# Turning the row maxima of both query halves with one product, and moving that product inside a layer-2 slot

## The chip, the core and the metric

One core of one Trainium2 chip runs the whole program. The metric is device time in microseconds (us); the median of the timed runs is compared. The engines named below are PE (TensorE, with its weight loads shown as PEld), DVE (VectorE), ACT (ScalarE), POOL (GpSimd) and SP (SyncE, which issues most DMAs).

## The reference

Two cross-attention layers, one after the other, on x of shape (16, 256, 320) with a context of shape (16, 256, 512). Each layer has 20 heads of 16 channels. The last 4 context tokens are image tokens, the first ones text. Layer 1 treats 77 tokens as text and all the others as image tokens; layer 2 treats 252 as text and 4 as image.

```python
# layer 1, cut
q = x @ Wq;  k_text = text @ Wk;  v_text = text @ Wv          # text = context[:, :77]
probs = softmax(q_h @ k_h^T * scale);  text_out = probs @ v_h
scores = q_h @ ip_k_h^T * scale                                # ip = context[:, 77:]
text_probs = softmax(q @ k_text^T * scale)                     # over all heads at once
sem = (text_probs @ text) @ ip^T * scale
ip_probs = softmax(scores + 0.5 * sem) * spatial_mask
out = (text_out + ip_probs @ ip_v_h) @ Wout + bout + x
# layer 2, cut (text = context[:, :252], ip = context[:, 252:])
probs_t = softmax(q @ k_t^T * scale);  text_out = probs_t @ v_t
qsem = l2norm(probs_t @ text);  sem = qsem @ l2norm(ip)^T
probs_ip = softmax(q @ k_ip^T * scale + 0.5 * sem) * spatial_mask
out = (text_out + probs_ip @ v_ip) @ W_out + b_out + x
```

Every softmax over tokens needs the row maximum of its scores per query and head; that is what this change is about.

## The kernel before

The work is cut into groups of 4 heads of one batch: 16 batches x 5 groups = 80 groups per layer (NS = 80), and one group is handled in one *slot*. Slots 0 to 79 are layer 1 (`slot0`), 80 to 159 layer 2 (`slot1`). The 256 queries of a batch are worked in two halves of 128 (t = 0, 1).

For a group the kernel computes the scores twice. The first time queries lie on the partitions (`score0`, L772; in layer 2 the second loop of `both1`, L922), only to get the row maxima with DVE (L773 and L774 for the text and image part in layer 1, L923 in layer 2). The second time tokens lie on the partitions (`turned0`, L795; in layer 2 the first loop of `both1`, L917), and there the maxima enter as extra rows of the stacked operand Q, so that ACT's exponential (L798, L929) can read the scores out of PSUM with the maximum already subtracted. To become rows of Q, the maxima have to be turned: a product with the identity puts them on a few partitions (`maxima0`, L780; `maxima1`, L955), ACT copies that to the tile mt (L782, L957), and a small DMA issued by ACT writes mt into Q (L783, L959). The tile mn with the maxima has one part per query half, and each half has a product of its own.

A layer-1 slot k runs, in PE's order: `maxima0` for group k+1, the scores of group k+2 for half 0, `turned0` of group k for half 0, fill, `attend0` of group k-1 (L833, the weighted values), the scores of group k+2 for half 1, `turned0` for half 1, fill. A layer-2 slot k runs: `both1` half 0 (L917 for group k, L922 for group k+2), `attend1` of group k-2 (L988 and L990, into the values' bank pv of tag P), `both1` half 1, then the norm products of group k-1 (`norm1`, L975, in four portions with fill between them), and at its end `maxima1` for group k+2. POOL multiplies and subtracts on the probabilities (L801, L966).

*Fill* is everything that is not per group: projections of queries, keys and values (L260, L632), the semantic scores of layer 1 (L690 to L719), closing a batch (`close0`, `close1`), loading and splitting weights (weights1 to weights8). These are generators, and the table `STEPS` says for each of their steps at which time (counted in slots, relative to the batch or to the start of layer 2) it is run; `fill` runs the steps that are due. PE's order is always the written one. In layer 1 a scheduler orders ACT, DVE, POOL and SP; in layer 2 only SP's queue.

PSUM has 8 banks: 2 of tag T (turned scores), 1 of tag P (the values' bank), 3 of tag X (all else, taken in a ring by `bank()`), and S (2 banks, one tile) for the scores. `late` keeps back an instruction until `settled` or `release`, `hold` begins such a stretch.

Of the kernel before, what the change touches and what calls it, by code (L numbers as in the profile page):

```python
# [9 lines left out]
FR = mybir.dt.float32r  # L10
# [6 lines left out]
B = 16  # L17
# [22 lines left out]
LEAD = 4  # L40

# [8 lines left out]
def xattn2(  # L50
# [714 lines left out]
    def score0(k, t):  # L765
        Q, K = QK[k]
        if t == 0:
            maxes[k] = buf("mn", [128, 2, 2, 4], FR, bufs=2)
        mn = maxes[k]
        sp = scores()  # L770
        for h in range(4):
            mm(sp[:, h], Q[: XROW + T0, h, t * 128 : (t + 1) * 128], K[: XROW + T0, h], start=True, stop=True)  # L772
        nc.vector.tensor_reduce(mn[:, t, 0], sp[:, :, :T0], axis=AX.X, op=ALU.max)  # L773
        anchor(nc.vector.tensor_reduce(mn[:, t, 1], sp[:, :, T0:], axis=AX.X, op=ALU.max))  # L774

    def maxima0(k, queue=nc.scalar):
        Q, mn = QK[k][0], maxes[k]
        mp = bank()
        for t in range(2):
            mm(mp[:8, t * 128 : (t + 1) * 128], mn[:, t].rearrange("p a h -> p (a h)"), ident_r, start=True, stop=True)  # L780
        mt = buf("mt", [8, S], FR)
        casts.append(nc.scalar.copy(mt, mp[:8, :S]))  # L782
# [120 lines left out]
    def both1(k, t):  # L903
# [3 lines left out]
        if a:  # L907
            if t == 0:
                maxes[k + 2] = buf("mn", [128, 4, 4], FR, bufs=2)[:, :2]
# [8 lines left out]
        if a:  # L918
# [4 lines left out]
            anchor(nc.vector.tensor_reduce(maxes[k + 2][:, t], sp[:, :, :T1], axis=AX.X, op=ALU.max))  # L923
# [27 lines left out]
    def maxima1(k):  # L951
        mn = maxes[k]
        mp = bank()
        for t in range(2):
            mm(mp[:4, t * 128 : (t + 1) * 128], mn[:, t], ident_r, start=True, stop=True)  # L955
        mt = buf("mt", [8, S], FR)[:4]
        nc.scalar.copy(mt, mp[:4, :S])  # L957
# [35 lines left out]
    def slot1(k):  # L993
        last = k - 1 if NS < k <= 2 * NS else None
        mine = k < 2 * NS
        if k == NS:
# [4 lines left out]
        summed = []  # L1001
# [3 lines left out]
        yield lambda: both1(k, 1)  # L1005
        if last:
# [19 lines left out]
        yield lambda: maxima(k + 2)  # L1026
# [153 lines left out]
    def first_keys():  # L1180
# [5 lines left out]
    STEPS = {  # L1186
        "k1": (-7, -6.2, -6.2, -5, -4.2, -3.4,),
        "t1": (-3.2, -2.2, -2.2, -1.4, -0.2,),
        "o1": (-7, -6.8, -6, -5.8, -4, -3.4,),
        "i1": (6.8, 7.6, 7.6, 8.8, 9.4, 9.6, 10.6, 10.8, 10.8, 12.2,),  # L1190
        "c1": (12.8, 12.8, 13.4, 14, 14, 15.8,),
        ("i1", B - 2): (6.6, 7, 7.2, 7.2, 7.8, 8, 8.6, 9.2, 9.2, 9.6,),
        ("c1", B - 2): (9.8, 11.8, 11.8, 12.2, 12.4, 12.4,),
        ("i1", B - 1): (6.8, 7.6, 7.8, 10, 10, 10, 11, 11, 11.2, 12,),
        ("c1", B - 1): (12.2, 13, 13, 13.2, 13.4, 16,),
# [16 lines left out]
        ("c0", B - 1): (5.8, 5.8, 6.4, 7, 7.2, 8,),  # L1212
# [257 lines left out]
```

## Time and profile before

| | |
|---|---|
| timed runs | 1476.69 us median, 1475.23 to 1477.35 |
| profiled execution, first to last instruction | 1475.7 us span; its own time is not listed apart from the runs above |
| PE busy | 97% of the span |
| DVE, POOL, ACT busy | 79%, 78%, 65% |
| granted TensorE clock, mean | 0.993 |
| DMA | 211.78 MB, 144 GB/s on average |

The profile is of one execution. Busy times are sums over the span; matmuls overlap with each other, so for PE the time from the start of one instruction to the start of the next says more than the length of one. The "idle before" of a row is time in which the engine waited, with the event that ended it. Shapes like 128*8 128x128 in a matmul's row are the stationary side and the moving side.

### The profile page before, as it was taken

To read this page: it belongs to the slowest core of one execution; us is meant where nothing else is said; L and a number is where in the kernel's file an instruction comes from. 1 tells how busy PE (TensorE), PEld (TensorE's weight loads), DVE (VectorE), ACT (ScalarE), POOL (GpSimd) and SP (SyncE) were. 2 spreads that over 40 slices of the span, in tenths; PEclk is the share of its full clock that TensorE was granted. 3 is DMA by queue.
4 is the path that set the end of the run, shared out by engine and by line. 5 is a ranking of instruction groups with operands and counts; after the bars stand their busy time and mean duration, and the time that the engine had idled before them with its cause. 6 is when DMAs were issued, how large, how long until landed. Compare 5 with 4: busy or idle time off the path is not lost.

```text
span 1475.7 us, 35302 instructions
## 1 busy us (share of the span) xinstructions
PE 1433.6 (97%) x12438; PEld 1186.7 (80%) x12438; DVE 1166.0 (79%) x2569; ACT 956.5 (65%) x2074; POOL 1151.8 (78%) x1173
## 2 busy tenths in 40 slices
PE   6899999999999999799999999999999999999998
PEld 6788888888888878687778887888888888888865
DVE  5487676777677787967888888888888888888897
ACT  5577676767676776756666566656665666566553
POOL 4179797979797877987788877787778877887785
PEclk9999999999999999999999999999999999999999
DMA  6756565656656577565434433543354345433511
GB/s 196 194 160 184 134 184 141 184 143 165 162 154 164 144 195 205 140 184 158 138 102 140 146 119 101 161 146 102 118 161 146 89 131 161 135 101 116 150 32 50
DMA packets 230667, 211.78 MB, mean 144 GB/s; under 512 B 56314, under 2 KB 217116, under 8 KB 230492
## 3 DMA queue, kind: packets, MB, share of 16 engines
q1 hardware_dynamic: 229222, 208.56, 50.3%
q8 instruction: 99, 1.62, 0.5%
q10 hardware_dynamic: 1270, 0.98, 0.2%
q14 instruction: 76, 0.62, 0.1%
HBM read 122.07 MB, written 86.44 MB: 141 GB/s over the span
## 4 chain that ended last, share of the span: by engine, by line
PE 86%; DMA 4%; DVE 3%; POOL 3%; ACT 2%; issue 1%; SPq 0%; ACTq 0%; DVEq 0%; POOLq 0%
PE X L260 22%; PE X L975 18%; PE X L632 11%; PE P L833 7%; PE S L772 5%; PE P L988 5%; PE T L917 5%; PE T L795 4%; PE S L922 3%; PE P L990 2%; DMA kd<-kst 2%; PE X L1108 1%; POOL P L801 1%; PE X L690 1%; POOL wt L966 1%
## 5 line engine op out<-in xcount | busy, mean ns | idle before, releaser
L801 POOL TENSOR_TENSOR P<-P,rs 128x512 f32<-128x512 f32 x320 | 413.6, 1316 | 140.2 <-ACT P L798 140.2
L975 PE MATMUL X<-ctb,gm 128*128 128x512 f32 x1120 | 295.3, 407 | 0.0
L966 POOL TENSOR_TENSOR wt<-P,ctb 128x512 f32<-128x512 f32 x212 | 268.6, 1296 | 0.0
L923 DVE TENSOR_REDUCE mn<-S 128x4 fp32r<-128x1008 f32 x160 | 192.8, 1205 | 81.0 <-PE S L922 79.4
L975 PEld LDWEIGHTS X<-ctb,gm 128*128 128x128 f32 x1120 | 203.6, 190 | 49.4 <-issue 0.4
L798 ACT ACTIVATE P<-T 128x512 f32<-128x512 f32 x320 | 174.7, 593 | 100.5 <-PE T L795 81.0
L978 DVE TENSOR_TENSOR wt<-X,wt 128x512 f32<-128x512 f32 x240 | 159.3, 681 | 4.9 <-PE X L975 4.9
L929 ACT ACTIVATE P<-T 128x512 f32<-128x512 f32 x212 | 115.0, 597 | 54.5 <-PE T L917 41.6
L980 POOL TENSOR_TENSOR wt<-wt 128x512 f32<-128x512 f32 x80 | 103.6, 1295 | 58.3 <-DVE wt L978 58.3
L965 ACT ACTIVATE ctb<-P 128x512 fp32r<-128x512 f32 x212 | 122.5, 625 | 32.7 <-PE X L975 31.1
L774 DVE TENSOR_REDUCE mn<-S 128x4 fp32r<-128x716 f32 x160 | 142.4, 890 | 0.0
L833 PE MATMUL P<-P,vr 128*32 128x256 f32 x1920 | 123.8, 387 | 1.8 <-DVE tmp L850 0.8
L632 PE MATMUL X<-hq,wE 128*128 128x256 f32 x768 | 111.1, 289 | 4.4 <-ACT hq L615 3.9
L260 PE MATMUL X<-cta,wA 128*128 128x252 f32 (+3 forms) x726 | 104.2, 289 | 6.9 <-ACT wA L187 6.8
L632 PE MATMUL X<-ho,wF 128*128 128x256 f32 x768 | 106.6, 284 | 0.9 <-DVE ho L871 0.6
L632 PEld LDWEIGHTS X<-hq,wE 128*128 128x128 f32 x768 | 101.6, 195 | 7.2 <-ACT hq L615 4.4
L260 PEld LDWEIGHTS X<-cta,wA 128*128 128x128 f32 (+1 forms) x726 | 94.4, 191 | 10.7 <-ACT wA L187 7.0
L632 PEld LDWEIGHTS X<-ho,wF 128*128 128x128 f32 x768 | 98.7, 189 | 3.9 <-DVE ho L871 1.0
L844 DVE STREAM_TRANSPOSE nt<-P 128x512 f32<-128x512 f32 x80 | 57.0, 713 | 44.2 <-PE P L833 43.9
L773 DVE TENSOR_REDUCE mn<-S 128x4 fp32r<-128x308 f32 x160 | 74.5, 466 | 21.5 <-PE S L772 21.1
L833 PEld LDWEIGHTS P<-P,vr 128*32 128x32 f32 x1920 | 55.7, 110 | 42.7 <-issue 6.0
L772 PE MATMUL S<-ks,qs 125*128 125x256 f32 x480 | 87.0, 304 | 0.9 <-DVE mn L774 0.8
(223 smaller groups left out, 3279.7 us busy)
## 6 DMA issues: line engine op xcount, KB each, us to landing
qd<-q SPq DMA_DIRECT2D x48, 384.0 KB
kd<-kst SPq DMA_DIRECT2D x66, 256.0 KB
rawc<-in_cT_dram SPq DMA_DIRECT2D x60, 256.0 KB
qs<-qd SPq DMA_DIRECT2D x160, 96.0 KB
ks<-kd SPq DMA_DIRECT2D x160, 96.0 KB
qs<-qd SPq DMA_DIRECT2D x60, 192.0 KB
ks<-kd SPq DMA_DIRECT2D x60, 192.0 KB
qd<-q SPq DMA_DIRECT2D x32, 256.0 KB
```

The source lines that it names most:

```text
L260: last = mm(out, lhs(a, k), rhs(b, k), start=i == 0, stop=i == len(terms) - 1)
L632: mm(pp, w(s, k, slice(m * 128, (m + 1) * 128)), a[:, t], start=i == 0, stop=i == len(terms) - 1)
L772: mm(sp[:, h], Q[: XROW + T0, h, t * 128 : (t + 1) * 128], K[: XROW + T0, h], start=True, stop=True)
L774: anchor(nc.vector.tensor_reduce(mn[:, t, 1], sp[:, :, T0:], axis=AX.X, op=ALU.max))
L798: exp = anchor(nc.scalar.activation(pt, st[p], AF.Exp, scale=SCALE))
L801: anchor(nc.gpsimd.tensor_mul(pt, pt, rs[:, t : t + 1].to_broadcast([128, 2, S])))
L833: mm(pv[32 * s : 32 * s + 32, o : o + S], v[:, vt, h : h + 32], P[k, s // 2][:, t, s % 2], start=vt < 2, stop=vt != 1,)
L923: anchor(nc.vector.tensor_reduce(maxes[k + 2][:, t], sp[:, :, :T1], axis=AX.X, op=ALU.max))
L965: nc.scalar.activation(R[k, u][:, t], P[k, u][:, t], AF.Copy, scale=0.5)
L966: anchor(nc.gpsimd.tensor_sub(W[k, u][:, t], P[k, u][:, t], f(R[k, u][:, t])))
L975: mm(yp, gm[:, gb], R[k, u][:, kt], start=i == 0, stop=i == len(blocks[n]) - 1)
L978: nc.vector.tensor_mul(product, yp, w[:, n])
```

## The change

The maxima of both halves go into one tile mn in which the half is the last, fastest index. One product then turns all of them: its stationary side has 16 columns (8 in layer 2) instead of two products with 8 (4) columns each, its result has 128 columns instead of 256 on twice the partitions, and so have the copy to mt and the source of the DMA. What lands in Q is the same.

In layer 2 the product for group k+1 is now issued in slot k right behind `both1` half 1, where it was issued for group k+2 at the end of slot k. It goes into columns 384 to 511 of the values' bank that `attend1` of the same slot has just filled (columns 0 to 255), and takes no bank of the X ring. Its DMA is no longer kept back.

Besides, the table `STEPS` is moved to the top of the file, and some of its times change.

```diff
     def score0(k, t):
...
-            maxes[k] = buf("mn", [128, 2, 2, 4], FR, bufs=2)
+            maxes[k] = buf("mn", [128, 2, 4, 2], FR, bufs=2)
...
-        nc.vector.tensor_reduce(mn[:, t, 0], sp[:, :, :T0], axis=AX.X, op=ALU.max)
-        anchor(nc.vector.tensor_reduce(mn[:, t, 1], sp[:, :, T0:], axis=AX.X, op=ALU.max))
+        nc.vector.tensor_reduce(mn[:, 0, :, t], sp[:, :, :T0], axis=AX.X, op=ALU.max)
+        anchor(nc.vector.tensor_reduce(mn[:, 1, :, t], sp[:, :, T0:], axis=AX.X, op=ALU.max))
 
     def maxima0(k, queue=nc.scalar):
         Q, mn = QK[k][0], maxes[k]
-        mp = bank()
-        for t in range(2):
-            mm(mp[:8, t * 128 : (t + 1) * 128], mn[:, t].rearrange("p a h -> p (a h)"), ident_r, start=True, stop=True)
-        mt = buf("mt", [8, S], FR)
-        casts.append(nc.scalar.copy(mt, mp[:8, :S]))
+        mp = bank()[:16, :128]
+        mm(mp, mn.rearrange("p a h t -> p (a h t)"), ident_r, start=True, stop=True)
+        mt = buf("mt", [16, 128], FR)
+        casts.append(nc.scalar.copy(mt, mp))
...
-    def maxima1(k):
+    def maxima1(k, into=None):
         mn = maxes[k]
-        mp = bank()
-        for t in range(2):
-            mm(mp[:4, t * 128 : (t + 1) * 128], mn[:, t], ident_r, start=True, stop=True)
-        mt = buf("mt", [8, S], FR)[:4]
-        nc.scalar.copy(mt, mp[:4, :S])
+        mp = bank()[:8, :128] if into is None else into[:8, 384:]
+        mm(mp, mn.rearrange("p c t -> p (c t)"), ident_r, start=True, stop=True)
+        mt = buf("mt", [8, 128], FR)
+        nc.scalar.copy(mt, mp)
...
     def slot1(k):
...
         yield lambda: both1(k, 1)
+        if k > NS:
+            yield lambda: maxima(k + 1, *[x[2] for x in summed])
...
         yield 0.8
-        yield lambda: maxima(k + 2)
         yield lambda: stacks(k + LEAD)
...
-        for b, t, o in (... (d, (-2.4, -1.4, -1, -0.8, -0.4, 0, 1.2), ...)):
+    "s0o": (-2.4, -1.4, -1, -0.8, -0.4, 0.4, 1.6,),
-        "o1": (-7, -6.8, -6, -5.8, -4, -3.4,),
+    "o1": (-7, -6.8, -6, -5.8, -5.4, -3.4,),
```

The other times that change are: the second and third step of the values of even batches (0.2 later); queries 3, values 2, semantic scores 3 and close 0 at the start of layer 1; weights1, weights6, weights3 and weights8 around the end of layer 1; o1 of batch 0; the last batch's c1.

In the rows below, L826, L833, L848, L772, L773 and L686 of the changed file are L772, L780, L795, L718, L719 and L632 of the file before. On PE in layer 1, around the maxima of slot 42, the order before was:

```order
L772 MATMUL S<-ksl,qsl 128x256 x4
L795 MATMUL T<-qs_187,ks_191 128x256 x4
L632 MATMUL X<-hq_293,wE_85 128x256 x8
L780 MATMUL X<-ident_r,mn_556 8x128 x2
L772 MATMUL S<-ks_190,qs_186 128x256 x4
```

and now it is:

```order
L826 MATMUL S<-ksl,qsl 128x256 x4
L848 MATMUL T<-qs_187,ks_191 128x256 x4
L772 MATMUL X<-tph_449,M_333 128x256
L773 MATMUL X<-tph_449,M_333 128x256
L772 MATMUL X<-tph_449,M_333 128x256
L773 MATMUL X<-tph_449,M_333 128x256
L686 MATMUL X<-hq_293,wE_85 128x256 x8
L833 MATMUL X<-ident_r,mn_556 16x128
L826 MATMUL S<-ks_190,qs_186 128x256 x4
```

The four products of the odd batch's last semantic step (tph with M) stood half a slot earlier, ahead of `attend0`; they now stand behind `turned0`, and the pair of turning products has become one.

On PE in layer 2, in slot 114 from `both1` half 1 on, the order before was (ctb and gm are operands of `norm1`, hq and wE of a query projection, cta and wA of a key projection):

```order
L917 MATMUL T<-qs_188,ks_192 128x256 x4
L922 MATMUL S<-ks_190,qs_186 128x256 x4
L975 MATMUL X<-ctb_82,gm 128x512 x4
L632 MATMUL X<-hq_293,wE_85 128x256 x8
L975 MATMUL X<-ctb_82,gm 128x512 x3
L975 MATMUL X<-ctb_83,gm 128x512 x7
L955 MATMUL X<-ident_r,mn_555 4x128 x2
L260 MATMUL X<-cta_80,wA_84 128x252 x6
```

and now it is (L970, L975, L1007, L1027 and L314 of the changed file are L917, L922, L955, L975 and L260 before):

```order
L970 MATMUL T<-qs_188,ks_192 128x256 x4
L975 MATMUL S<-ks_190,qs_186 128x256 x4
L1007 MATMUL P<-ident_r,mn_556 8x128
L1027 MATMUL X<-ctb_82,gm 128x512 x4
L686 MATMUL X<-hq_293,wE_85 128x256 x8
L1027 MATMUL X<-ctb_82,gm 128x512 x3
L1027 MATMUL X<-ctb_83,gm 128x512 x4
L686 MATMUL X<-hq_293,wE_85 128x256 x8
L1027 MATMUL X<-ctb_83,gm 128x512 x3
L314 MATMUL X<-cta_80,wA_84 128x252 x6
```

The turning product has moved from behind the norm products to ahead of them, from a bank of tag X to the values' bank, and one portion of the query projection (step five of o1) has come into this slot from the next.

On ACT in the same slot, from the second half's exponentials on, the order before was:

```order
L929 ACTIVATE P_93<-T 128x512
L929 ACTIVATE P_94<-T 128x512
L640 CAST q_297<-X 128x256
L965 ACTIVATE ctb_82<-P_93 128x512 x2
L965 ACTIVATE ctb_83<-P_94 128x512 x2
L607 ACTIVATE gm<-gm 128x128
L957 CAST mt_196<-X 4x256
L959 DMA qs_186<-mt_196 2x2x256
L562 CAST kst_235<-X 128x252
```

and now it is (L982, L1009, L1011, L694, L1017, L661 and L616 are L929, L957, L959, L640, L965, L607 and L562 before):

```order
L982 ACTIVATE P_93<-T 128x512
L982 ACTIVATE P_94<-T 128x512
L1009 CAST mt_196<-P 8x128
L1011 DMA qs_188<-mt_196 2x4x128
L694 CAST q_297<-X 128x256
L1017 ACTIVATE ctb_82<-P_93 128x512 x2
L694 CAST q_297<-X 128x256
L1017 ACTIVATE ctb_83<-P_94 128x512 x2
L661 ACTIVATE gm<-gm 128x128
L616 CAST kst_235<-X 128x252
```

The copy to mt and its DMA have moved from the slot's end to right behind the exponentials, ahead of the casts to ctb.

More of the change, by code (lines that the diff above doesn't have):

```diff
@@ L908, in both1 @@
             if t == 0:
-                maxes[k + 2] = buf("mn", [128, 4, 4], FR, bufs=2)[:, :2]
+                maxes[k + 2] = buf("mn", [128, 4, 2], FR, bufs=2)
             sp = scores()
@@ L922, in both1 @@
                     mm(sp[:, 2 * u + j], a[0][rows, j, t * 128 : (t + 1) * 128], a[1][rows, j], start=True, stop=True)
-            anchor(nc.vector.tensor_reduce(maxes[k + 2][:, t], sp[:, :, :T1], axis=AX.X, op=ALU.max))
+            anchor(nc.vector.tensor_reduce(maxes[k + 2][:, :, t], sp[:, :, :T1], axis=AX.X, op=ALU.max))
             image_scores(k + 2 - NS, t, sp)
@@ L995, in slot1 @@
         mine = k < 2 * NS
+        summed = []
         if k == NS:
@@ L1276, in ahead, with maxima @@
             both1(k - 2, t)
-    def maxima(k):
+    def maxima(k, *into):
         if k < 2 * NS:
-            (maxima0 if k < NS else maxima1)(k)
+            if k < NS:
+                maxima0(k)
+            else:
+                maxima1(k, *into)
     def part(*key):
```

49 lines of the change are left out of this document (29 added, 20 removed), and 58 rows, old and new, of the table STEPS.

## The prediction

> **What bounds the kernel now.** I read the page's first part, then the busy time by stretches, then the waits of TensorE (PE), and only then single slots in the timeline. The page:
>
> ```profile
> PE 1433.6 (97%) x12438; PEld 1186.7 (80%) x12438; DVE 1166.0 (79%) x2569; ACT 956.5 (65%) x2074; POOL 1151.8 (78%) x1173
> ...
> q10 hardware_dynamic: 1270, 0.98, 0.2%
> ```
>
> The stretches are layer 1 and layer 2 without the start and the end (columns: length; then PE, PEld, DVE, ACT and POOL busy; clock; DMA):
>
> ```profile
> 48.00:660.00 612.00, 592.74 (x5519) 509.41 (x5518) 450.46 (x1058) 432.01 (x937) 493.85 (x437) 0.99 0.63 168
> 660.00:1440.00 780.00, 775.20 (x6505) 621.73 (x6505) 666.00 (x1385) 484.49 (x1049) 620.61 (x669) 1.00 0.42 126
> ```
>
> In layer 2 PE is idle for 4.8 of 780 us, and the next engine, DVE, is busy for 85%. In layer 1 PE is idle for 19 of 612 us. The chain of waits names what those idle times are, first for PE in layer 2 alone, then the two entries that belong to the maxima in the whole run (us in total, times, longest):
>
> ```profile
> PE S L922 <- DVE sr L939: 2.3, 4, 0.8
> PE P L990 <- DVE wt L980: 1.3, 2, 1.1
> PE X L955 <- DVE kst L564: 0.6, 1, 0.6
> PE T L917 <- DVE ho L871: 0.5, 1, 0.5
> ...
> PEld X L780 <- DVE mn L774: 7.4, 11, 1.7
> ...
> PE X L780 <- DVE mn L774: 3.7, 4, 1.4
> ```
>
> So PE's own instruction stream sets the time; a matmul taken out of it is time taken out, unless it ran inside a wait. A wait matters where PE stands in it, and nowhere else.
>
> **The change part by part.** *One product for two.* The groups by shape, and one turn of maxima in each layer (start, length, engine, line, xcount):
>
> ```profile
> L780 PE MATMUL X<-ident_r,mn 128*8 128x128 f32 x160 | 24.8, 225 | 5.1 <-DVE mn L774 3.7 <-DMA kd<-kst 0.3 <-DVE ho L871 0.3
> L955 PE MATMUL X<-ident_r,mn 128*4 128x128 f32 x160 | 22.9, 223 | 0.6 <-DVE kst L564 0.6
> ...
> 404.31 0.29 PE L780 MATMUL X<-ident_r,mn 128*8 128x128 f32 x2
> 404.43 0.68 PE L772 MATMUL S<-ksl,qsl 125*128 125x256 f32 x4
> ...
> 1009.72 0.40 PE L922 MATMUL S<-ks,qs 48*128 48x256 f32 x4
> 1010.05 1.19 PE L975 MATMUL X<-ctb,gm 128*128 128x512 f32 x4
> 1011.08 1.11 PE L632 MATMUL X<-hq,wE 128*128 128x256 f32 x8
> 1012.03 2.49 PE L975 MATMUL X<-ctb,gm 128*128 128x512 f32 x10
> 1014.37 0.28 PE L955 MATMUL X<-ident_r,mn 128*4 128x128 f32 x2
> 1014.48 1.60 PE L260 MATMUL X<-cta,wA 128*128 128x252 f32 x12
> 1016.01 0.51 PE L917 MATMUL T<-qs,ks 49*128 49x256 f32 x4
> ```
>
> The mean of 225 ns is latency and overlaps with neighbours; what counts is start to start. Two products take 0.12 us in layer 1 (404.31 to 404.43) and 0.11 in layer 2 (1014.37 to 1014.48), so one product is 0.06 and 0.055 us of PE's stream. The 128 moving columns stay the same when the stationary side grows from 8 or 4 columns to 16 or 8, so one of each pair goes. In layer 2 that is 80 x 0.055 = 4.4 us. In layer 1 at most 15 of the 80 pairs stood in a wait for DVE (11 weight loads and 4 matmuls, in the rows above); there nothing is saved by this, and 65 x 0.06 = 3.9 us remain.
>
> The Trainium skill (TensorE: Matmul & The Clock Gate, Back-to-back issue gap) gives about 81 ns for a 128-column matmul in a stream in which every matmul has its own weight load. By that figure the same 145 products would be 11.7 us instead of 8.3, and the sum below 14.0; I keep the 55 to 60 ns that the trace has for these very products.
>
> *The new place in layer 2.* The product now stands between the second scores (L922, a half-height product of 48 rows) and norm1 (L975, full height). A change of shape costs here: L922's four matmuls run two by two, and 256 columns take 0.12 us from start to start (609.77 to 609.89 in a row below), so two pairs should take 0.24, yet L975 starts 0.33 after them; and L975's first four then take 1.03 us where ten take 2.34, that is 0.94 for four. The change of shape is thus worth 0.09 + 0.09 = 0.18 us, paid once per slot before and, if the product counts as full height like L975, once after. I take no change. The bounds are a product that hides the 0.18 (gain 14 us over 80 slots at most, and 7 if only one half hides) and one that pays it a second time (loss 14 us).
>
> *Copy and transfer.* The copy to mt moves 128 elements per partition instead of 256:
>
> ```profile
> L782 ACT CAST mt<-X 8x256 fp32r<-8x256 f32 x80 | 28.4, 356 | 2.1 <-PE X L780 2.0
> ...
> L562 ACT CAST kst<-X 128x252 fp32r<-128x252 f32 x48 | 17.8, 371 | 52.5 <-PE X L260 51.1 <-DMA rawc<-in_wo_dram 0.8 <-PE T L917 0.6
> ...
> L692 ACT COPY sp<-X 128x77 f32<-128x77 f32 x32 | 6.7, 234 | 4.1 <-PE X L690 4.0
> ...
> 1009.92 1.09 ACT L929 ACTIVATE P<-T 128x512 f32<-128x512 f32 x2 [1.02 <-PE T L917]
> 1012.23 0.37 ACT L640 CAST q<-X 128x256 fp32r<-128x256 f32 x1 [1.23 <-PE X L632]
> ...
> 54.27 0.70 SPq L783 DMA_DIRECT2D qs<-mt  x1
> ...
> 56.38 1.20 PE L795 MATMUL T<-qs,ks 127*128 127x256 f32 x4 [4.63 <-DMA qs<-mt]
> ```
>
> Between 77 columns at 234 ns and 252 at 371 the copy should take about 275 ns instead of 356: 13 us less on ACT in all, off the path, so nothing. In layer 2 the copy and its DMA issue now sit behind the exponentials of the second half. Queued behind them on ACT are the casts to ctb and whatever fills the slot; ACT stood idle there for 1.23 us (1011.01 to 1012.23), which covers a copy of 0.28 and an issue of 0.5 to 0.7. If that cover were gone, the casts would come 0.8 us later, and their reader on PE is norm1 one slot on. SP and POOL queues are not passed, since the issue is ACT's. The transfer has the same bytes in twice as many pieces; its queue has 0.2% of the DMA time, so its share is nothing even doubled.
>
> The new deadline is the first L917 of the next slot, which needs the row in Q. From the second scores (1009.72) to that L917 (1016.01) there are 6.29 us. The chain is the exponentials (end 1011.01), copy 0.28, and 2.11 from issue to use (54.27 to 56.38): 1013.4, with 2.6 us to spare. Before, the row had more than a slot. In the values' bank the next attend1 must also wait for this copy, which ends some 5 us earlier; and one allocation of the X ring per slot is gone, which the waits above show nobody standing in: nothing for either. DVE's reduces write the same 4 elements with a stride of two against the 308 to 1008 that they read: nothing.
>
> *The steps.* In layer 1 the four products L718/L719 of the odd batch move from ahead of attend0 to behind turned0, directly ahead of the next product of maxima or with one projection between:
>
> ```profile
> 156.17 0.55 PE L780 MATMUL X<-ident_r,mn 128*8 128x128 f32 x2
> ...
> 457.66 0.55 PE L780 MATMUL X<-ident_r,mn 128*8 128x128 f32 x2
> ...
> 381.68 0.89 DVE L774 TENSOR_REDUCE mn<-S 128x4 fp32r<-128x716 f32 x1
> ...
> 609.77 0.28 PE L718 MATMUL X<-tph,M 77*128 77x256 f32 x1
> 609.89 0.28 PE L719 MATMUL X<-tph,M 77*128 77x256 f32 x1
> ...
> 612.83 0.22 PE L780 MATMUL X<-ident_r,mn 128*8 128x128 f32 x1
> 614.28 0.23 PE L780 MATMUL X<-ident_r,mn 128*8 128x128 f32 x1 [1.23 <-DVE mn L774]
> ...
> 598.92 0.62 ACT L187 CAST wB<-rawc 128x512 fp32r<-128x512 f32 x1 [1.54 <-DMA rawc<-in_wvi_dram]
> ...
> 601.50 0.74 PE L709 MATMUL X<-ident,sp 128*77 128x128 f32 x2 [2.94 <-ACT sp L705]
> ```
>
> In that slot a pair spans 0.55 instead of 0.29, five times (first and last row), because DVE's reduce ends late (382.57 in the instance at 382.30): a wait of 0.26. Four products of 0.12 are 0.48 of work put into it, so the wait goes with the spared product: 5 x (0.26 + 0.06) = 1.6 us. What is late next there is attend0, which gets 0.48 less work ahead of it; PE stands in no wait for POOL's P of any size in the rows above, so I take nothing. At 612.83 the same move fills 0.48 of a wait of 1.4: 0.5 us.
>
> The largest wait is L709's 2.94 us, behind ACT, which itself stood for a weight load (598.92). L709 moves one slot later, past it. But the third weight cast moves up too, ahead of the first half's exponentials, and still needs that load; then L795 of the second half waits for them. I take nothing, between a gain of 4.6 (the wait of 2.9 and the half-speed spell behind it, below) and a loss of as much. The other moved steps (queries, values and close of the first batches, o1, the last c1) keep PE's amount of work and fill no wait that I can place: nothing, within 1 us.
>
> ```profile
> 601.50:605.00 3.50, 3.50 (x20) 2.73 (x24) 1.71 (x3) 2.57 (x7) 2.60 (x4) 0.51 0.18 55
> ```
>
> That row is the stretch after the wait: the granted clock was 0.51 for 3.5 us, which costs 1.7 us on top of the wait.
>
> **Sum:** 4.4 + 3.9 + 1.6 + 0.5 = 10.4 us. The profiled execution's span is 1475.7, so 1465.3; the median of the runs is 1.0 above that span, so 1466.3.
>
> **The rivals.**
>
> *The product pays a change of shape of its own* and the kernel ends slower. For it: its stationary side is 8 columns, not 128. Against it: at 1014.37 the pair stands between full-size products, and 0.11 us for both leaves no room for any such cost. Priced at 0.18 in 80 slots, 14.4 us more than the sum: 1480.7. It decides from 10.4/80 = 0.13 us per slot. The Trainium skill (TensorEngine Tiling, Key Properties) says that a change of tiling mode drains TensorE, which speaks against a small product put right behind row-tiled ones; the trace agrees for L922 to L975, and shows none for the old place of the product.
>
> *The maxima's row comes late* in layer 2, since it starts 0.6 of a slot later. It would have to use up the 2.6 us to spare; from 2.7 us of delay in each slot it eats the gain. Only short slots at the end come near: about 1467.
>
> *The gain is eaten elsewhere,* DVE or POOL becoming what PE waits for: DVE's 85% and PE's 4.8 us in layer 2 speak against it. Only the layer-1 waits would go: 1474.6.
>
> *The step table loses at the layers' border:* a wait of 2.9 us and one more half-speed spell: 1470.9.
>
> *The product hides the change of shape,* one half in all slots: 7 us more, 1459.
>
> **How the numbers follow.** The sum as forecast 0.62; the border loses 0.14; the shape is hidden 0.09; eaten elsewhere 0.06; own change of shape 0.05; late row that costs more than the gain 0.04. A measurement of this kernel tells changes of more than about 0.2%, 3 us, from none. Faster: 0.62 + 0.14 + 0.09 = 0.85; within 0.2%: 0.06; slower: 0.09. The range reaches from the hidden shape with a little more, 1457, to the border's loss with 2.6 us for the small terms that I took at nothing, 1473.5, and leaves out the last three cases and the far end of the hidden shape.
>
> **What would show it.** Right: PE has 160 matmuls of L780 and L955's successors instead of 320, the pairs at 156 to 458 us no longer span 0.55, layer 2 is shorter by 4 to 5 us with PE idle for about 5, and the gap from the second scores to norm1 grows by 0.06. Wrong: that gap grows by 0.2 (own change of shape) or not at all (hidden); L917 appears as waiting for the DMA of mt (late row); PE's idle time in layer 2 grows by the 4 us saved (eaten); new waits of 2 to 3 us or half-clock stretches between 580 and 690 us (border).

## The result and the profile after

The changed kernel takes 1468.82 us (median of 4 runs, 1466.53 to 1470.27), the kernel before 1477.02 in the same comparison (1475.23 to 1478.32): ratio 0.9945, 95% interval 0.9931 to 0.996. That is 8.2 us faster, where I had forecast 10.4 below a median of 1476.7. In the profiled executions the span goes from 1475.7 to 1468.2.

In everything below, lines are those of the changed file: L833, L826, L848, L886 and L314 are the old L780, L772, L795, L833 and L260, and in layer 2 L970, L975, L1007, L1027 and L686 are the old L917, L922, L955, L975 and L632. First the engines and the queue of mt from the page after:

```profile
PE 1419.4 (97%) x12278; PEld 1175.4 (80%) x12278; DVE 1181.5 (80%) x2569; ACT 939.1 (64%) x2074; POOL 1151.6 (78%) x1173
...
q10 hardware_dynamic: 2222, 0.98, 0.3%
```

PE has 160 matmuls fewer, as it should. DVE does the same 2569 instructions as before and yet is busy for 15.5 us longer (1166.0 before); 14.9 of it are in one line, L672, the last step of preparing hq, the operand of a query projection; e11 comes back to it. The two layers without start and end, in the columns of the prediction's table:

```profile
48.00:660.00 612.00, 588.12 (x5468) 504.99 (x5467) 459.46 (x1061) 426.51 (x940) 494.45 (x438) 0.99 0.63 167
660.00:1440.00 780.00, 772.07 (x6458) 619.77 (x6451) 677.45 (x1391) 478.08 (x1056) 624.78 (x675) 0.99 0.42 126
```

PE's idle time did not stay put: 23.9 us instead of 19.3 in layer 1, and 7.9 instead of 4.8 in layer 2. Part of what the stream lost in work came back as waits. The groups of the product and of its copy:

```profile
L833 PE MATMUL X<-ident_r,mn 128*16 128x128 f32 x80 | 17.9, 223 | 7.9 <-DVE mn L828 5.4 <-ACT P L851 1.5 <-DVE tph L766 0.4
L1007 PE MATMUL P<-ident_r,mn 128*8 128x128 f32 x77 | 17.5, 227 | 0.0
...
L835 ACT CAST mt<-X 16x128 fp32r<-16x128 f32 x80 | 19.7, 247 | 2.5 <-PE X L833 2.5
L1009 ACT CAST mt<-P 8x128 fp32r<-8x128 f32 x77 | 18.3, 238 | 0.7 <-PE P L1007 0.7
```

In layer 2 PE never waited in front of the product in its new place (0.0 in 77). In layer 1 it waited for DVE's reduce 5.4 us in all, more than the 3.7 that the two products had together. And this is PE in a slot of layer 2, to be laid beside the slot at 1009.72 of the prediction:

```profile
1007.79 0.40 PE L975 MATMUL S<-ks,qs 48*128 48x256 f32 x4
1008.12 0.23 PE L1007 MATMUL P<-ident_r,mn 128*8 128x128 f32 x1
1008.18 1.15 PE L1027 MATMUL X<-ctb,gm 128*128 128x512 f32 x4
1009.17 1.12 PE L686 MATMUL X<-hq,wE 128*128 128x256 f32 x8
```

From the second scores to norm1 it is now 0.39 us instead of 0.33, which is the 0.06 that the prediction named as its sign. But the four matmuls of norm1 then take 0.99 us (1008.18 to 1009.17) instead of 1.03 (1010.05 to 1011.08). Medians over the 62 slots in which at least seven norm1 matmuls follow, in ns from start to start:

```
                     last score -> product -> product -> norm1 1st -> 2nd -> 3rd
before                        206 ------------------------->     340      234
after                         207 -> 63 ------------------>      286      232
two products (below)          206 -> 64 ------> 60 ------>       286      233
```

A norm1 behind a full-height projection takes 231 ns from its first to its second matmul (29 cases). Behind the half-height scores it takes 340, and behind the product 286. So the product costs 63 and gives back 54: in its new place it is almost free. Its old place was dearer than the one slot of the prediction shows: in 24 of the 60 slots from 11 to 71 it stood straight ahead of the half-height scores of the next slot. There it took 0.99 us on average from the last instruction ahead of the first L917 to the first L922 (1.00 in e1 below, with one product), against 0.88 behind a projection.

How far each kernel is ahead of the kernel before is read from the start of `attend0` in layer 1 (counted from the first one) and of a slot's first L917 or L970 in layer 2, in one profiled execution of each (us, minus is ahead). The runs are named as in the experiments below:

```
slot            before's   after  after   e1     e2     e9     e3     e5     e6     e7
                 start            again  one    moved  +o1    table  early  border both
layer 1, 0        71.99   -2.61  -2.60  -0.73  -2.58  -1.28  -1.00  -2.77  -1.95  -1.29
layer 1, 5       110.86   -0.74  -1.97  -1.58  -3.19  -1.82  -0.98  -4.31  -1.30  -2.28
layer 1, 10      152.72   +3.06  -2.62  -1.87  -3.47  -2.11  -1.39  -1.93  -1.95  -2.57
layer 1, 50      454.21   -1.03  -6.67  -3.15  -4.75  -3.34  -3.74  -6.49  -6.04  -7.10
layer 1, 60      532.14   -2.75  -8.38  -3.52  -3.47  -2.10  -4.70  -8.17  -7.77  -8.79
layer 2, 0       672.32   -2.54  -7.61  -2.61  -4.02  -0.33  -1.59  -5.48  -7.74  -8.50
layer 2, 11      777.46   +0.65  -4.45  -1.14  -2.06  +3.13  +0.65  -4.26  -4.23  -6.11
layer 2, 71     1373.27   -7.01 -12.19  -3.87  -5.43  -4.53  +0.81  -11.58 -11.88 -13.72
end (span)      1475.70   -7.54 -12.72  -2.53  -5.74  -5.02  -0.36  -13.15 -13.45 -15.29
```

The profiled execution of e3 (1477.12 us) is the second shortest of its nine runs, and its median is 5.2 us longer.

The change gained steadily where nothing stalls: 4.09 us in 40 slots of layer 1 and 7.66 in 60 of layer 2, 0.102 and 0.128 us per slot. It lost in three places: 1.9 us between slots 0 and 5 of layer 1, 3.8 between slots 5 and 10, and 3.2 between slots 0 and 11 of layer 2.

### The profile page after: what moved, and what is told of

Same layout as the page of the kernel before. It is cut to its first block, busy times and chain, and to the rows that moved or that the text cites. A ratio compares the mean times of both kernels' runs of the same rounds, so it can differ in the third digit from the quotient of the medians.

```text
span 1468.2 us, 35025 instructions
## 1 busy us (share of the span) xinstructions
PE 1419.4 (97%) x12278; PEld 1175.4 (80%) x12278; DVE 1181.5 (80%) x2569; ACT 939.1 (64%) x2074; POOL 1151.6 (78%) x1173
## 4 chain that ended last, share of the span: by engine, by line
PE 88%; DVE 4%; POOL 3%; issue 2%; DMA 2%; ACT 1%; SPq 0%; ACTq 0%; DVEq 0%; POOLq 0%
PE X L314 23%; PE X L1027 18%; PE X L686 12%; PE P L886 7%; PE S L826 6%; PE P L1040 5%; PE T L848 5%; PE T L970 4%; PE S L975 3%; PE P L1042 2%; PE X L1161 1%; PE X L744 1%; POOL P L854 1%; PE P L1007 1%; POOL wt L1018 1%
## 5 line engine op out<-in xcount | busy, mean ns | idle before, releaser
L854 POOL TENSOR_TENSOR P<-P,rs 128x512 f32<-128x512 f32 x320 | 411.9, 1311 | 141.0 <-ACT P L851 140.8
L1027 PE MATMUL X<-ctb,gm 128*128 128x512 f32 x1120 | 295.9, 406 | 0.0
L1027 PEld LDWEIGHTS X<-ctb,gm 128*128 128x128 f32 x1120 | 204.6, 192 | 38.2 <-issue 0.4
L982 ACT ACTIVATE P<-T 128x512 f32<-128x512 f32 x212 | 115.2, 597 | 58.4 <-PE T L970 56.6
L1017 ACT ACTIVATE ctb<-P 128x512 fp32r<-128x512 f32 x212 | 122.5, 625 | 29.4 <-PE X L1027 17.4
L886 PE MATMUL P<-P,vr 128*32 128x256 f32 x1920 | 124.9, 389 | 3.6 <-DVE sp L747 3.3
L686 PE MATMUL X<-hq,wE 128*128 128x256 f32 x768 | 109.4, 287 | 4.7 <-ACT hq L669 3.7
L686 PE MATMUL X<-ho,wF 128*128 128x256 f32 x768 | 108.9, 286 | 3.6 <-DVE ho L926 2.2
L686 PEld LDWEIGHTS X<-hq,wE 128*128 128x128 f32 x768 | 102.9, 194 | 8.5 <-ACT hq L669 4.2
L314 PE MATMUL X<-cta,wA 128*128 128x252 f32 (+3 forms) x726 | 103.1, 288 | 6.3 <-ACT wA L241 5.9
L686 PEld LDWEIGHTS X<-ho,wF 128*128 128x128 f32 x768 | 100.5, 189 | 10.2 <-DVE ho L926 3.7
L314 PEld LDWEIGHTS X<-cta,wA 128*128 128x128 f32 (+1 forms) x726 | 95.4, 191 | 11.2 <-ACT wA L241 6.2
L886 PEld LDWEIGHTS P<-P,vr 128*32 128x32 f32 x1920 | 56.2, 111 | 45.0 <-issue 4.7
L826 PE MATMUL S<-ks,qs 125*128 125x256 f32 x480 | 86.3, 302 | 0.6 <-DVE mn L828 0.6
```

The costliest lines, as they stand in the source:

```text
L314: last = mm(out, lhs(a, k), rhs(b, k), start=i == 0, stop=i == len(terms) - 1)
L686: mm(pp, w(s, k, slice(m * 128, (m + 1) * 128)), a[:, t], start=i == 0, stop=i == len(terms) - 1)
L854: anchor(nc.gpsimd.tensor_mul(pt, pt, rs[:, t : t + 1].to_broadcast([128, 2, S])))
L886: mm(pv[32 * s : 32 * s + 32, o : o + S], v[:, vt, h : h + 32], P[k, s // 2][:, t, s % 2], start=vt < 2, stop=vt != 1,)
L1017: nc.scalar.activation(R[k, u][:, t], P[k, u][:, t], AF.Copy, scale=0.5)
L1027: mm(yp, gm[:, gb], R[k, u][:, kt], start=i == 0, stop=i == len(blocks[n]) - 1)
```

## The experiments

Each kernel ran beside the kernel before on the same chip, whose median there was 1475.9 to 1476.3 us.

**e1: one product in the old places, old step table.** The kernel after with the old numbers in `STEPS`, and in layer 2

```
-        if k > NS:
-            yield lambda: maxima(k + 1, *[x[2] for x in summed])      # behind both1, half 1
...
         yield 0.8
+        yield lambda: maxima(k + 2)                                   # the slot's end, a bank of its own
         yield lambda: stacks(k + LEAD)
```

> The kernel before with one product in the place of two in both layers; in layer 2 it stays at the end of the slot with a bank of its own, and the step table stays as it was. Theory: a product in its old place costs PE 0.055 to 0.06 us from start to start in both layers, so 80 x 0.055 = 4.4 and 65 x 0.06 = 3.9 us go: 1477.0 - 8.3 = 1468.7. Rival 1, the product runs in the shadow of its neighbours and the gain of the whole change comes from the step table: 1477, within 1.5. Rival 2, the new place in layer 2 is what pays there: only layer 1 gains, 1473.

Measured: 1476.96 us, ratio 1.0006 (0.9993 to 1.002). The theory fell: sparing 160 products alone gave nothing that can be told from no change. In the profiled execution, slots 10 to 50 of layer 1 gain 1.28 us, 0.032 each, and slots 11 to 71 of layer 2 gain 2.73, 0.046 each, some 6 us over all slots. In layer 1 half of a product's time came back in front of the one that stayed: the 20 gaps from a projection to the product in slots 10 to 50 grew from 2.35 to 4.00 us in sum, since DVE's reduce ends when it did. The rest did not last: in that execution 0.9 us are lost between slot 60 of layer 1 and slot 0 of layer 2, 1.5 from there to slot 11 and 1.3 behind slot 71, and the median is another 1.8 us above it (the 11 runs lie between 1473.5 and 1483.2).

**e2: the product moved too, old step table.** The kernel after, with only the numbers in `STEPS` as before.

> As the first run, and in layer 2 the product stands behind the second scores and writes into the values' bank; the step table is still the old one. Theory: the trace after the change shows that the second matmul of norm1 starts 0.680 us after the first of the second scores with the product between them and 0.670 without, so in the new place the product costs 0.01 us instead of 0.06 and what follows the old place is rid of it: some 0.07 us in each of 80 slots, 5.6 us below the first run, 1463. Rival 1, the place is worth nothing and the 0.13 us per slot that layer 2 gained come half from the step table: as the first run, 1468.7. Rival 2, the late row makes the next slot's first products wait: 1470 or more, with waits of L970 for the transfer of mt.

Measured: 1470.83 us, ratio 0.9963 (0.9951 to 0.9975). That is 6.1 us below e1, near the 5.6 of the theory, but not for its reason: norm1's second matmul does come after 286 ns, as in the table of gaps, yet the slope in layer 2 is only 0.056 us per slot against e1's 0.046, and the rest of the difference lies outside these slots. The waits of PE from 760 to 1400 us show why the slope stays behind; in e2 they are this one entry,

```profile
PE X L314 <- DVE wt L1030: 0.9, 6, 0.2
```

which the trace after does not have. Projections behind norm1 stand for a bank that DVE still reads: the 48 gaps from norm1 to L314 between slots 11 and 71 are 14.66 us in e2 and 11.11 after, with 0.5 us in place of 0.23 once in each of 12 batches.

**e9: e2 with the new fifth step of o1.**

```
-    "o1": (-7, -6.8, -6, -5.8, -4, -3.4,),
+    "o1": (-7, -6.8, -6, -5.8, -5.4, -3.4,),
```

> One product moved behind the second scores with the old step table but for the fifth step of o1 in batches 2 to 15, which is the new one. Theory: in the run without it each batch of layer 2 has a wait of about 0.3 us ahead of a projection of L314, six of them named for DVE's wt, which the trace after has not; the step takes it away, 0.36 us in each of 14 batches: 1470.8 - 5.0 = 1465.8, with a slope of -0.13 us per slot in layer 2 against before instead of -0.056. Rival: the slope stays at -0.056 and the other rows of the table remove the wait: 1470.8.

Measured: 1469.2 us, ratio 0.9949 (0.9934 to 0.9965). The mechanism is as the theory says: the same 48 gaps are 11.11 us again, the entry above is gone, and from slot 11 to 71 it gains 7.66 us, 0.128 per slot, as the kernel after does. The total is 3.4 us short of the theory; the profiled execution stalled more at the border, where it loses 6.5 us from slot 50 of layer 1 to slot 11 of layer 2 and e2 2.7. So the step of o1, which I had costed at nothing, removes a wait that the new place makes. With the products in their old places it brings nothing: in e3, which has it too, slots 11 to 71 lose 0.2 us. (The medians of e2 and e9 alone, with overlapping intervals, would not show this.)

**e3: the new step table alone.** The kernel before with the new numbers in `STEPS`.

> The kernel before with the new step table alone, all products as before. Theory: the table loses. It takes 2 us of waits from layer 1, but the early batches lose 4 us (a wait of 3.3 us at attend0 and a half-clock stretch of 3.4) and the start of layer 2 loses 3.4 (two more half-clock stretches): 1477 + 5 = 1482. Rival 1, as my forecast had it, the table gains 2 us: 1475. Rival 2, the losses come from the spared products shifting the slots against each other, not from the table: 1477, within 1.5.

Measured: 1482.27 us, ratio 1.0033 (1.0022 to 1.0045): slower, as the theory said. Its trace bears out only part of the reason: from slot 0 to 10 of layer 1 nothing is lost (-1.00 to -1.39), from slot 0 to 11 of layer 2 it is 2.2 us. Where the longer runs lose the rest is not shown. In slots 10 to 50 of layer 1 the table gains 2.35 us; with e1's 1.28 that is 3.6 of the 4.09 of the whole change.

**e8: two products in the new place.**

```
-        mm(mp, mn.rearrange("p c t -> p (c t)"), ident_r, start=True, stop=True)
+        for i in range(1 if into is None else 2):
+            mm(mp, mn.rearrange("p c t -> p (c t)"), ident_r, start=True, stop=True)
```

> The kernel after with the product in layer 2 issued twice, both behind the second scores and into the same place of the values' bank. Theory: from the second scores to the second matmul of norm1 a fixed time passes for the change of shape, 0.67 us, and what fits under it is free; two products of 0.06 fit nearly, so the second costs about 0.01 to 0.02 us a slot: 1468.8 + 1 = 1470. Rival 1, one product alone is hidden and the second costs its full 0.06: 80 x 0.06 = 4.8 us, 1473.6. Rival 2, a small product has a change of shape of its own and each costs 0.1 or more: 1477.

Measured: 1471.87 us, ratio 0.9975 (0.9961 to 0.9989). The theory of a fixed time fell, rival 1 holds: in the table of gaps above the second product adds its full 60 ns, and norm1 behind it still takes 286. Slots 11 to 71 gain 4.41 us instead of 7.66, 0.054 less per slot. Only the first product is hidden. Why 54 ns stay behind one product or two was not found.

**e4: the new place with a bank of its own.**

```
-            yield lambda: maxima(k + 1, *[x[2] for x in summed])
+            yield lambda: maxima(k + 1)
```

> The kernel after, but the product in layer 2 writes into a bank of its own from the X ring instead of the values' bank; its place stays behind the second scores. Theory: the bank is worth nothing, the place alone hides the product: as the kernel after in this comparison, within 2 us, with 63 ns from the product to norm1 and 285 from norm1's first to its second matmul, and -0.13 us per slot in layer 2 against before. Rival: one more allocation of the X ring per slot makes norm1 or a projection wait for a bank: 80 x 0.05 = 4 us more and a slope of -0.08 or less.

Measured: 1508.17 us, ratio 1.0218 (1.0196 to 1.024): the rival, ten times as large. The gaps at the product are the same (63 and 288 ns). Most of what is lost stands in its waits of PE from 760 to 1400 us; the second fence has one of them from its timeline:

```profile
PE X L314 <- DVE wt L1032: 17.6, 12, 1.5
PE X L1161 <- DVE wt L1030: 2.7, 12, 0.3
```

```profile
792.70 2.74 PE L314 MATMUL X<-wC,cta 128*128 128x320 f32 x12 [1.47 <-DVE wt L1032]
```

Once per batch a projection now gets the bank that DVE still reads for the last norm product, and four of these waits were followed by 3.4 us at half clock. With this table of steps, the place hides the product only as long as it takes no bank of the ring. Whether other times for the projections would avoid these waits was not tried.

**e5, e6, e7: parts of the table as before.** In the kernel after, e5 has the old rows of the first batches, e6 those of the weights at the border, e7 both:

```
-    ("q0", 3): (5, 6.2, 7, 8.2, 9,),          +    ("q0", 3): (5, 6.2, 7, 7.2, 8,),              # e5, e7
-    ("v0", 2): (1.8, 3.4, 4,),                +    ("v0", 2): (2.8, 4.4, 5,),
...                                                 # also s0 of batch 3 and c0 of batch 0
-    ("w3", 1): (0.2,),                        +    ("w3", 1): (1.6,),                            # e6, e7
...                                                 # also w1, w6, w3 0, w8 and o1 of batch 0
```

> The kernel after with the four rows of the step table for the first batches of layer 1 (q0 of batch 3, v0 of 2, s0 of 3, c0 of 0) as before. Theory: these rows bring two waits of 1.2 us and a half-clock stretch between 65 and 105 us, some 3 us; the 3.3 us wait at 133 us in the trace after is an event of that one execution, since the run with two products in layer 2 has the same layer 1 and did not show it. So 1468.8 - 3 = 1466. Rival: the rows only move work between the first slots, the waits come from the spared product: 1468.8 within 1.5, and the offset of slot 5 to slot 0 stays at +1.2 to +1.9 us against before.

> The kernel after with the rows of the step table for the weights at the border of the layers (w1, w6, w3, w8, o1 of batch 0) as before. Theory: these rows bring the wait of 1.3 us and the half-clock stretch at 734 us, 3 us from slot 2 to slot 7 of layer 2, against a gain of up to 1.5 us around slot 60 of layer 1: 1468.8 - 2 = 1467. Rival 1: the stretches come from the new place of the product, and the rows cost nothing: 1468.8. Rival 2: the rows gain on the whole, as they remove the wait of 2.9 us at 601 us: 1472.

> The kernel after with both groups of rows as before; what stays of the new table are the odd batches' s0, the even ones' v0, the o1 of batches 2 to 15 and the last c1. Theory: the two losses add, 1468.8 - 3 - 2 = 1464. Rival: the half-clock stretches are dealt anew in each program, and nothing adds: 1467 to 1470.

Measured: e5 1465.04 us, 0.9928 (0.9909 to 0.9947); e6 1464.35, 0.9921 (0.9904 to 0.9939); e7 1462.32, 0.9906 (0.9889 to 0.9922). The two single intervals overlap that of the kernel after; e7's does not. e7 is the best version, 6.5 us below the change and 13.6 below the kernel before. From slot 0 to slot 5 of layer 1 the early rows cost 0.6 to 1.9 us in the three profiles that have them and all of the change (after, again, e6), against gains of 1.0 and 1.5 without them (e7, e5): that loss is shown. It belongs to the rows together with the spared products, since e3, which has the rows alone, neither gains nor loses there. The border rows are not: from slot 60 of layer 1 to slot 11 of layer 2, e6 loses 3.5 us and the kernel after 3.4 (3.9 again), with the same wait of 1.3 us for wt in the first slots of layer 2. What e6's profile gained against the first trace after it gained elsewhere, 4.4 us of it between slots 5 and 10, where the two run the same steps. So rival 1 holds for the rows at this place, and why e6's median is 4.5 us below that of the kernel after is not shown.

**e11: the kernel after once more.**

> The kernel after as it stands, in the same comparison as the last two runs, to see which stalls of its first trace return. Theory: the wait of 3.3 us at 133 us (DVE's L672 held for 4.9 us while POOL works without a break) does not return, the waits of 1.2 us at 90 and 103 us, those at 677 to 680 and 732 us and their half-clock stretches do: 1466 to 1469. Rival: the wait at 133 us belongs to this program and returns: 1469 to 1471.

Measured: 1469.47 us, ratio 0.9952 (0.9934 to 0.997): the median lies where the rival put it, but the profiled execution (1465.09) is the shortest of its seven runs, so whether the wait at 133 us stands in the longer ones is not shown. In this execution, 12.7 us shorter than before's, it did not return; the waits of 1.2 us at 88 and 101 us and those at the start of layer 2 did. The two traces of one program part by 1.2 us up to slot 5, where the first has one more half-clock stretch (at 68.46 us), and by 4.5 us from slot 5 to slot 10. There they differ in one DVE instruction. In the first:

```profile
129.54 5.00 POOL L854 TENSOR_TENSOR P<-P,rs 128x512 f32<-128x512 f32 x4
131.50 4.95 DVE L672 SCALAR_TENSOR_TENSOR hq<-hq,tmask,xq 128x256 fp32r<-128x256 f32 x1
...
134.50 1.25 POOL L670 TENSOR_TENSOR hq<-xq,hq 128x512 fp32r<-128x512 f32 x1
135.72 0.44 POOL L908 TENSOR_TENSOR hsn<-tmp 128x128 f32<-128x128 f32 x1
...
136.83 2.79 PE L886 MATMUL P<-P,vr 128*32 128x256 f32 x24 [3.31 <-DVE sp L747]
```

and again:

```profile
128.30 5.21 POOL L854 TENSOR_TENSOR P<-P,rs 128x512 f32<-128x512 f32 x4
130.28 0.84 DVE L672 SCALAR_TENSOR_TENSOR hq<-hq,tmask,xq 128x256 fp32r<-128x256 f32 x1
```

In the first execution L672 ends only 0.3 us after POOL's run of six instructions (135.72 + 0.44), everything behind it on DVE is late, and `attend0` waits until DVE has got to L747. In the second L672 ends inside POOL's first four. In e5's profile it took 3.68 us and PE waited 2.04. The Trainium skill (SBUF — State Buffer, SBUF: two separate sides) says that a DVE operation with two SBUF inputs and a GpSimd operation that reads SBUF lock each other out for a whole instruction. The traces agree, and show that it can be more than one: in the first execution L672 got in neither behind the second L854, in which it started, nor behind the next three instructions, only behind the fifth, L908.

The same pair is the 14.9 us of DVE's busy time. Once per batch of layer 2, L672 (L618 before) starts beside POOL's L670 (L616). Before:

```profile
1000.69 1.30 POOL L616 TENSOR_TENSOR hq<-xq,hq 128x512 fp32r<-128x512 f32 x1 [2.53 <-ACT hq L615]
1001.79 0.48 DVE L618 SCALAR_TENSOR_TENSOR hq<-hq,tmask,xq 128x256 fp32r<-128x256 f32 x1
```

and after:

```profile
999.45 1.30 POOL L670 TENSOR_TENSOR hq<-xq,hq 128x512 fp32r<-128x512 f32 x1 [2.94 <-ACT hq L669]
999.87 1.17 DVE L672 SCALAR_TENSOR_TENSOR hq<-hq,tmask,xq 128x256 fp32r<-128x256 f32 x1
```

In both it ends 0.3 us after POOL's instruction, whenever it began. The median over the last 13 batches is 0.49 us before, in e1 and in e3, and 1.1 us or more in every kernel with the product behind the second scores, so the new place brings it. PE does not pay for it there: after, its only wait from 760 to 1400 us is one of 0.3 us. No run changed these two instructions alone; that they exclude each other is what the rows and the page suggest, not what an experiment isolated.

**e10 and e12: the same move in layer 1.** If a change of shape hides a product, `attend0` with its 32-column tiles should do so too: in e7 the scores behind it come 309 ns after it, and their second matmul 223 instead of 118 ns after the first. Both start from e7:

```
         if k > 0:
-            yield lambda: maxima(k + 1)                    # head of the slot
             yield lambda: stacks(k + LEAD - 1, "M")
...
             yield lambda: attend0(k - 1)
-            yield lambda: stacks(k + LEAD - 1, "T")        # e10: to behind turned0(k, 1); e12: stays here
+            yield lambda: maxima(k + 1)
```

> The kernel with both groups of rows as before (median 1462.3), and the product of layer 1 moved from the head of the slot to behind attend0, ahead of the second scores; the copy of the query rows (T) goes behind the second turned scores, so that the exponentials keep their place on ACT. Theory: behind attend0, whose tiles have 32 columns, the scores pay for a change of shape as norm1 does: 309 ns to the first and 223 instead of 118 to the second. A product at the head costs 0.060 itself and 0.055 more in the scores behind it (173 instead of 118); behind attend0 it costs 0.060 less 0.050. So 0.105 us in each of 77 slots, 8 us, and the 3 us of waits of L833 for DVE's reduce go too: 1452 to 1455. Rival 1: the change of shape there hides nothing, and only the waits go: 1459. Rival 2: the row of maxima comes late (copy 0.25, 2.1 us from issue to landing, 4.3 us from the product to the first turned scores of the next slot), and L848 waits for the transfer of mt: 1465 or more.

Measured: 1500.67 us, ratio 1.0179 (1.0154 to 1.0204): none of the cases. PE's gaps came out near the theory (309 to the product, 70 to the scores, then 171 instead of 223; at the head, behind a projection, 119 and 120 without the 55 extra). The order on ACT spoiled it, first entry of its waits:

```profile
PE S L826 <- ACT qs L795: 16.6, 24, 2.9
```

The query rows T are needed by the next slot's scores; I had moved them behind the exponentials as if they had time.

> The kernel with both groups of rows as before (median 1462.3) and the product of layer 1 behind attend0, as in the run of 1500.7, but with the copy of the query rows (T) where it was, ahead of the product on ACT. Theory: that run lost its time to the late T alone (L826 waits for ACT's L795 24 times, 16.6 us, and half-clock stretches behind them), while the product in its new place cost what I expected: 70 ns to the scores, then 171 instead of 223, and no 0.115 at the head. So 0.1 us in each of 77 slots below 1462.3, less some 3 us of waits for the row's transfer, which came in four slots: 1455 to 1459. Rival 1: the row is late in most slots now that the copy stands behind T, L848 waits for the transfer of mt: 1465 or more. Rival 2: another resource is short in layer 1, such as the X ring or DVE's reduces, and the slots stay 0.15 us longer than in the kernel it is made from: 1475 or more.

Measured: 1480.23 us, ratio 1.0027 (1.0005 to 1.0049). Its profiled execution, at 1492, is the longest of its twelve, so the sums below are upper ends. The waits for L795 are gone, and rival 1 has taken their place, first in the waits of PE, then at one place of the timeline:

```profile
PE T L848 <- DMA qs<-mt: 25.6, 13, 4.5
```

```profile
436.45 0.23 PE L833 MATMUL X<-ident_r,mn 128*16 128x128 f32 x1
438.06 0.25 ACT L835 CAST mt<-X 16x128 fp32r<-16x128 f32 x1
438.34 0.62 ACTq L836 DMA_DIRECT2D qs<-mt  x1
442.98 0.77 PE L848 MATMUL T<-qs,ks 127*128 127x256 f32 x2 [3.16 <-DMA qs<-mt]
```

The copy came 1.6 us after the product, behind T on ACT, and from issue to use it took 4.6 us, not the 2.1 that I had read from the one row at 54.27. From half a slot ahead the row comes too late in layer 1; of the places tried, only the head of the slot gives it time.

## Why the prediction was right, and where its terms were not

The direction and the range held: 1468.8 lies 2.5 us above the forecast of 1466.3. But that the sum came out so near is luck: its misses have opposite signs. At its slopes the change would gain 18.4 us over 2 x 80 slots, and what it lost at the start of each layer took much of it back.

*One product of each pair, layer 2 (forecast 4.4 us).* Mechanism right; e1 shows 0.046 instead of 0.055 per slot, 3.6 us over 80.

*The new place (forecast nothing, bounds of 14 either way).* This is the step that failed, the sentence "I take no change". The rival "the product hides the change of shape, one half in all slots" (chance 0.09, 7 us more) is what happened: 0.128 per slot after against 0.046 in e1, so 0.082 from the place together with the step of o1 that it needs, 6.6 us over 80. The hidden half is 0.054 of that, 4.3 us. The rest has to do with what the product left: I had written that the trace shows no change of shape for the old place, which is so at 1014.37, but not in the 24 of 60 slots where the product stood ahead of half-height scores (1.00 against 0.88 us in e1). Why these starts are slower, and how much of the 0.12 us the change kept, is not shown. The rows in front of me bore on it: 0.09 of the 0.18 us lay in norm1's own first matmuls, behind the place where the product was to stand. I had let the product pass that half on undiminished, and no row said so. In the new place the product pays no change of shape of its own, and the row of maxima is in time: no L970 waits for mt.

*The values' bank and o1 (forecast nothing).* Wrong in both. e4 shows that with a bank of the ring, and this table, the new place costs 39 us against the change itself, e9 against e2 that the step of o1 is worth 0.36 us per batch there. The prediction looked for waits in the trace before, where nobody stood for a bank of the ring; in e2 and e4 projections do, behind the moved product.

*Layer 1 (forecast 3.9 for the product, 1.6 and 0.5 for the moved L772 and L773).* The stage came out at 0.102 us per slot; my terms are 6.0 us, 0.075 per slot. The parts were off against each other: the product alone brought 0.032 (e1), since the reduce behind which it stands did not come earlier, and the table 0.059 (e3).

*The early steps (forecast within 1 us).* e5 and e7 against the kernel after show a loss of 1.6 to 3.4 us from slot 0 to slot 5.

*The border (forecast nothing, bounds 4.6).* The wait of 2.9 us did go: between slots 68 and 69 of layer 1, where it stood, the two traces after gain 2.7 and 2.3 us. But other waits came around it, such as one of 2.2 us of L686 for DVE's ho, and from slot 67 of layer 1 to slot 0 of layer 2 both lose, 0.6 and 1.1 us. Then comes a loss of 3.4 between slots 0 and 7 of layer 2, with these waits of PE in the whole run after:

```profile
PE S L975 <- DVE sr L992: 2.9, 6, 0.8
PE P L1042 <- DVE wt L1032: 2.5, 2, 1.3
...
PE T L970 <- DVE ho L924: 1.5, 2, 0.8
```

So the rival of the border was right about a loss there. e6 loses 3.7 us there, so the rows I suspected are not its cause. Neither the move nor the table can be singled out: counted to slot 11, where the change has lost 3.2, e1 loses 1.5, e2 2.0 and e3, with the table alone, 2.2. Which instruction of DVE makes these waits in layer 2's first slots is left open.

## What to carry to other kernels

Where a matrix multiplication changes its shape from half-height or narrow tiles to full ones, look at the second matmul behind the change too: if it is late, a small product that is needed anyway can stand there for almost nothing, once. Before moving it, follow its result to the deadline with the slowest transfer of that stage, not with one quick one, and ask whose PSUM bank it takes: here, with one and the same table of steps, the bank decided between a gain of 8 us and a loss of 32. And a table of steps tuned for one order is no neutral part of a change: undo it row group by row group.

## What was not expected of the hardware

The half-clock stretches lie on a fixed grid of 3.413 us: after, 136.73, 679.45 and 734.06 are 159 and 16 such windows apart. Most half-clock windows follow one in which PE idled for part of the time. In these rows (length; PE, PEld, DVE, ACT, POOL; clock) PE idles for 3.21 of 3.41 us, and for 1.86:

```profile
133.32:136.73 3.41, 0.20 (x2) 0.00 (x0) 3.41 (x3) 0.24 (x1) 2.85 (x3) 1.00 0.63 119
136.73:140.15 3.42, 3.32 (x27) 1.73 (x28) 2.54 (x10) 2.82 (x8) 1.81 (x2) 0.50 0.00 0
...
730.65:734.06 3.41, 1.55 (x15) 0.75 (x14) 2.95 (x6) 0.79 (x2) 3.41 (x3) 1.00 0.41 119
734.06:737.47 3.41, 3.41 (x12) 2.52 (x10) 2.25 (x4) 1.61 (x4) 0.45 (x2) 0.50 0.54 174
```

Over all these profiles, the first 5 us of a run aside, windows with 1.2 to 1.8 us of idle went both ways, and none with more stayed without a half-clock window behind it. Behind a window that itself ran at half clock, a second one came with as little as 0.34 us of idle (e1, 597.61). At 564.01 before one came with no idle time ahead, but behind 2.79 us of matmuls with only 64 moving columns (L260, kst and wB). The same happened in e9 at 562.63; in e2, where 2.78 us of these matmuls fell into one window, it did not, so their part in it is not shown. The grid does not start with the kernel: its first line lay between 0.2 and 3.1 us after the start, so the same waits can fall into one window or two, and 1.7 us of time come or go with it. That may be part of why one program's runs spread over 4 us and more. The Trainium skill (TensorE: Matmul & The Clock Gate, Part 1: The HAM clock gate) has the free-running window of 3413 ns, and the traces agree. The Trainium skill warns on the same page (Why this matters for your kernels) of PE gaps of about 3 us between bursts, while here waits of 1.31 and 0.55 us in one window (732.17 and 733.79) were enough.
